# Two attention blocks on eight images: convolutions and layer 1's attention as seven half-size products, weight factors and the next image's q, k, v in DRAM, stages reordered

## The chip, the cores and the metric

The kernel runs on one core of a Trainium2 chip. Its time is the device time of one execution in microseconds (us), and the time of a version is the median of its runs. All arithmetic is in fp32.

## The reference

For each of 8 images x of 512 channels by 1024 positions, two blocks follow each other. Cut to what matters:

```
h  = group_norm(x, 32 groups)                 # layer 0
q, k, v = Wq h + bq, Wk h + bk, Wv h + bv     # 8 heads of 64 channels
a  = softmax(q^T k / 8, over keys) applied to v, per head
x  = x + Wp a + bp

h  = group_norm(x, 8 groups)                  # layer 1: one head of 512 channels
q, k, v = Wq h + bq, Wk h + bk, Wv h + bv
x  = x + Wp (softmax(q^T k / sqrt(512)) v) + bp
```

Each "W h" is a product of 512x512 by 512x1024; layer 0's attention multiplies 64 channels by 1024x1024 scores for each head, layer 1's 512 channels by 1024x1024.

## The kernel before, in words

A prologue, `fold`, multiplies layer 1's weights together once: M (`wm`) from those of q and k, Z (`wz`) from those of v and p. Layer 1 then needs g = M h, scores g^T h, z = Z h, and values from z. So an image has six convolutions: v, q, k and p with layer 0's weights, g and z with layer 1's. The weights stay in SBUF as four 128-row slices each (`KC` = 4). 128 is the height of the array, 512 columns (`HT`) is the width of one product and of one PSUM bank, and 128x512 is the unit in which products are counted here: 32 per convolution, 64 each for layer 1's scores and values. In the trace one fp32 product is two records.

PSUM has two pools: `ps_sc`, three tiles of two banks, for scores, convolutions and the `sums` of the softmax, and `ps_acc`, two tiles of one bank, for the running `av` and small products.

Layer 0's attention goes over 4 pairs of heads times 2 halves of the positions: 8 units per image. In a unit two parts follow each other, each with four score tiles (L300, two heads beside each other), four exponentials on ScalarE (L307), additions of these on VectorE (L309, L311) and four products with v into `av` (L320). A unit is ended during the next one: `reciprocals` sums the exponentials over the partitions with `ones` (L268), VectorE takes the reciprocal (L272) and keeps the largest sum (L274), GpSimd keeps the reciprocals' sum (L275); the reciprocals go through DRAM (L277) and come back to all partitions (L281) as r; VectorE multiplies `av` by r (L330).

The loop over images runs: attention of layer 0, p mixed with the next image's v, layer 1's normalization, g (`by_channel`, L223), z (`by_token`, L239), layer 1's attention in two halves (L347, L362), then the next image's q and k. p adds to x at L407. PSUM results leave alternately by VectorE and ScalarE. While attention of layer 0 runs, the next image's normalization is done as `extra`. A scheduler places the instructions on each engine, by the order in which the program gives them out and the tiles that become free; a few products of the next stage go ahead of waiting ones. DMAs are issued by SP, in the prologue by ScalarE too.

At the end, `top_sums` and `all_recs` decide whether a general path, which isn't run with these data, must do the work again.

Of the kernel before, what the change touches and what calls it, by code (L numbers as in the profile page):

```python
# [15 lines left out]
P = 128  # L16
EPS = 1e-5

# [9 lines left out]
def two_attention_blocks_kernel(  # L28
# [41 lines left out]
    wsb = [const.tile([P, KC, C], F32, name=f"w{i}") for i in range(4)]  # L70

    wm = const.tile([P, KC, C], F32, name="wm")
    wz = const.tile([P, KC, C], F32, name="wz")
# [3 lines left out]

    class GroupNorm:  # L80
        def __init__(self, layer, xt, uid):
            self.layer, self.xt, self.uid = layer, xt, uid
            self.mv = small.tile([P, KC, 2], F32, tag="mv", name=f"mv_{uid}")

        def stats(self, c):
            st = small.tile([P, 2, 6], F32, tag="bnst", name=f"bnst_{self.uid}_{c}")
            for i in range(2):
                nc.vector.bn_stats(st[:, i, :], self.xt[c][:, ts(i, HT)])
            nc.vector.bn_aggr(self.mv[:, c, :], st)
# [27 lines left out]
        def apply(self, engine, dst, c):  # L117
            engine.tensor_scalar(dst, self.xt[c], self.s[:, c : c + 1], self.b[:, c : c + 1], ALU.mult, ALU.add)  # L118

    def main_path(ctx):  # L120
        imgs = ctx.enter_context(tc.tile_pool(name="img", bufs=12))
# [3 lines left out]
        def img(name):  # L125
            return imgs.tile([P, T], F32, tag="img", name=name)

        def load_x(b, c, what):
            t = img(f"{what}_{b}_{c}")
            nc.sync.dma_start(t, x[b, c * P : (c + 1) * P, :])  # L130
            return t
# [6 lines left out]


        def fold():  # L140
            with tc.tile_pool(name="raw", bufs=1) as rawpool, tc.tile_pool(name="nat", bufs=2) as natpool:
                raw = [rawpool.tile([P, KC, C], F32, name=f"raw{i}") for i in range(4)]

                def load(i):
                    for h in range(2):
                        nc.scalar.dma_start(
                            raw[i][:, ts(h, 2), :],
                            w[4 + i, ts(h, C // 2), :].rearrange("(kc p) o -> p kc o", p=P),
                        )

                load(1)
                load(0)
                first = [load_x(0, c, "h0") for c in range(KC)]
                load(2)
                load(3)
                for i in (2, 0, 1, 3):
                    nc.scalar.dma_start(wsb[i], w[i].rearrange("(kc p) o -> p kc o", p=P))


                def natural(wt, nm):  # L160
                    t = natpool.tile([P, KC, C], F32, tag="nat", name=f"nat_{nm}")
                    for o in range(KC):
                        pt = acc_tile(f"tr_w{nm}_{o}")
                        for kc in range(KC):
                            nc.tensor.transpose(pt[:, ts(kc, P)], wt[:, kc, ts(o, P)], ident)
                        if o % 2 == 0:
                            nc.vector.tensor_copy(t[:, o, :], pt)
                        else:
                            nc.scalar.copy(t[:, o, :], pt)
                    return t  # L170

                def product(dst, lhs, rhs, nm):
                    for ic in range(KC):
                        ps = acc_tile(f"ps_w{nm}_{ic}")
                        for kc in range(KC):
                            nc.tensor.matmul(  # L176
                                ps, lhs[:, kc, ts(ic, P)], rhs[:, kc, :], start=(kc == 0), stop=(kc == KC - 1)
                            )
                        nc.vector.tensor_copy(dst[:, ic, :], ps)

                def bias_product(dst, lhs, vec, add, nm):
                    for oc in range(KC):
                        ps = acc_tile(f"ps_b{nm}_{oc}")
                        for kc in range(KC):
                            nc.tensor.matmul(
                                ps[:, 0:1], lhs[:, kc, ts(oc, P)], pcol(vec, kc), start=(kc == 0), stop=(kc == KC - 1)
                            )
                        if add is None:
                            nc.vector.tensor_copy(dst[:, oc : oc + 1], ps[:, 0:1])
                        else:  # L190
                            nc.vector.tensor_add(dst[:, oc : oc + 1], ps[:, 0:1], pcol(add, oc))

                wk = natural(raw[1], "k")
                wq = natural(raw[0], "q")
                norm = GroupNorm(0, first, "0_0")
                for c in range(KC):
                    norm.stats(c)
                product(wm, wq, wk, "m")
                norm.group_mean(acc_tile("gmean_0_0")[:, :KC])
                bias_product(ubias, wk, "bq1", None, "u")  # L200
                norm.affine(acc_tile("gvar_0_0")[:, :KC])
                for c in range(KC):
                    norm.apply(nc.vector if c % 2 else nc.gpsimd, first[c], c)
                product(wz, natural(raw[2], "v"), raw[3], "z")
                bias_product(obias[1], raw[3], "bv1", "bp1", "o")
                bias_product(obias[0], wsb[3], "bv0", "bp0", "o0")
            return first

        h0 = fold()
        qkpool = ctx.enter_context(tc.tile_pool(name="qka", bufs=16))  # L210
        vpool = ctx.enter_context(tc.tile_pool(name="vz", bufs=16))
        epool = ctx.enter_context(tc.tile_pool(name="e", bufs=6))
        sumpool = ctx.enter_context(tc.tile_pool(name="sum", bufs=2))
        rpool = ctx.enter_context(tc.tile_pool(name="r", bufs=2))
        rowpool = ctx.enter_context(tc.tile_pool(name="rows", bufs=3, space=bass.MemoryType.DRAM))


        def by_channel(wt, h, oc, bias, name):
            ps = sc_tile(f"ps_{name}")
            out = []  # L220
            for th in range(2):
                for kc in range(KC):
                    nc.tensor.matmul(  # L223
                        ps[:, th, :], wt[:, kc, ts(oc, P)], h[kc][:, ts(th, HT)], start=(kc == 0), stop=(kc == KC - 1)
                    )
                t = qkpool.tile([P, HT], F32, tag="qka", name=f"{name}_{th}")
                if th == 0:
                    nc.vector.tensor_scalar(t, ps[:, th, :], bias, None, ALU.add)
                else:
                    nc.scalar.activation(t, ps[:, th, :], AF.Identity, bias=bias)  # L230
                out.append(t)
            return out

        def by_token(wt, h, s2, name, between=None):
            ps = sc_tile(f"ps_{name}")
            out = []
            for i in range(2):
                for kc in range(KC):
                    nc.tensor.matmul(  # L239
                        ps[:, i, :], h[kc][:, ts(2 * s2 + i, P)], wt[:, kc, :], start=(kc == 0), stop=(kc == KC - 1)  # L240
                    )
                if i == 0 and between is not None:
                    between()
                t = vpool.tile([P, C], F32, tag="vz", name=f"{name}_{i}")
                if i == 0:
                    nc.vector.tensor_copy(t, ps[:, i, :])  # L246
                else:
                    nc.scalar.copy(t, ps[:, i, :])
                out.append(t)
            return out  # L250

        def queries_keys0(b, h):
            q, k = {}, {}
            for oc in range(KC):
                q[oc, 0], q[oc, 1] = by_channel(wsb[0], h, oc, pcol("bq0", oc), f"q0_{b}_{oc}")
                k[oc, 0], k[oc, 1] = by_channel(wsb[1], h, oc, pcol("bk0", oc), f"k0_{b}_{oc}")
            return q, k

        def reciprocals(total, heads, uid):

            sums = sc_tile(f"sums_{uid}").rearrange("p a b -> p (a b)")[:, : heads * P]
            sums = sums.rearrange("p (a b) -> p a b", a=heads)
            for i in range(4):
                nc.tensor.matmul(  # L268
                    sums[ts(i, 32), :, :], ones[:, :32], total[:, :heads, ts(i, P)], start=True, stop=True
                )  # L270
# [14 lines left out]
        def attention0(b, q, k, v, extra):  # L285
# [47 lines left out]
            while extra:  # L333
                extra.pop(0)()
# [279 lines left out]
```

## Time and profile before

| | |
|---|---|
| median of 3 runs | 3315.55 us (3313.39 to 3318.15) |
| profiled execution | 3314.92 us |
| its span | 3313.0 us |
| TensorE clock granted, mean | 0.995 |
| TensorE busy | 3257.4 us |
| VectorE busy | 1208.9 us |
| ScalarE busy | 658.1 us |
| GpSimd busy | 195.2 us |
| DMA | 81.82 MB, mean 25 GB/s |

The span is the time from the first to the last instruction that the profiler recorded. Busy time doesn't count register, branch, semaphore and DMA-issuing instructions. In the chain that ended last each step is followed back to what released it; "issue" in it is time in which the profile shows no wait. A row of the waits gives the engine and line that waited, the instruction on which it waited, the total in us, how often, and the longest. "DVE" is VectorE, "ACT" ScalarE, "PE" TensorE, "PEld" its weight loads, "POOL" GpSimd, "SP" the engine that issues DMAs.

### The profile page before, as it was taken

To read this page: it belongs to the slowest core of one execution; us is meant where nothing else is said; L and a number is where in the kernel's file an instruction comes from. 1 tells how busy PE (TensorE), PEld (TensorE's weight loads), DVE (VectorE), ACT (ScalarE), POOL (GpSimd) and SP (SyncE) were. 2 spreads that over 40 slices of the span, in tenths; PEclk is the share of its full clock that TensorE was granted. 3 is DMA by queue.
4 is the path that set the end of the run, shared out by engine and by line. 5 is a ranking of instruction groups with operands and counts; after the bars stand their busy time and mean duration, and the time that the engine had idled before them with its cause. 6 is when DMAs were issued, how large, how long until landed. Compare 5 with 4: busy or idle time off the path is not lost.

```text
span 3313.0 us, 24829 instructions
## 1 busy us (share of the span) xinstructions
PE 3257.4 (98%) x10130; PEld 1345.5 (41%) x10130; DVE 1208.9 (36%) x1461; ACT 658.1 (20%) x743; POOL 195.2 (6%) x149
## 2 busy tenths in 40 slices
PE   6999999999999999999999999999999999999899
PEld 3433444334443444434443344433444334443343
DVE  3165122751227412373124721256212651117512
ACT  0042001421014110240003400043000430005210
POOL 0010000100002000010000200010000100000000
PEclk9999999999999999999999999999999999999999
DMA  4000011000100002000020000100001000000000
GB/s 179 0 14 13 0 42 42 15 12 0 57 26 17 10 0 77 9 17 7 10 73 7 17 3 16 67 11 17 0 16 67 11 16 0 33 25 15 12 0 33
DMA packets 36697, 81.82 MB, mean 25 GB/s; under 512 B 5024, under 2 KB 5856, under 8 KB 36576
## 3 DMA queue, kind: packets, MB, share of 16 engines
q1 hardware_dynamic: 31872, 71.62, 6.3%
q10 hardware_dynamic: 4704, 8.55, 0.7%
q8 instruction: 82, 1.34, 0.2%
q14 instruction: 39, 0.32, 0.0%
HBM read 63.07 MB, written 17.07 MB: 24 GB/s over the span
## 4 chain that ended last, share of the span: by engine, by line
PE 93%; issue 4%; DVE 2%; POOL 0%; ACT 0%; DMA 0%; SPq 0%; DVEq 0%; ACTq 0%; POOLq 0%
PE av L362 13%; PE sc L347 13%; PE sc L300 13%; PE av L320 12%; PE ps_z L239 7%; PE ps_k L223 7%; PE ps_q L223 7%; PE ps_g L223 7%; PE ps_v L239 6%; PE ps_p L403 6%; PE sums L268 1%; DVE sum L311 1%; DVE sum L309 0%; PE ps_wz L176 0%; DVE h L118 0%
## 5 line engine op out<-in xcount | busy, mean ns | idle before, releaser
L307 ACT ACTIVATE e<-sc 128x1024 f32<-128x1024 f32 x512 | 484.5, 1029 | 479.3 <-PE sc L300 479.3
L311 DVE TENSOR_TENSOR sum<-sum,e 128x1024 f32<-128x1024 f32 x384 | 477.7, 1244 | 99.2 <-ACT e L307 77.9
L300 PE MATMUL sc<-q,k 64*128 64x512 f32 x2048 | 478.2, 603 | 7.6 <-DVE top_sums L274 7.6
L320 PE MATMUL av<-e,v 128*64 128x512 f32 x2048 | 467.7, 598 | 0.0
L362 PE MATMUL av<-e,z 128*128 128x512 f32 x1024 | 446.3, 594 | 0.0
L347 PE MATMUL sc<-g,h 128*128 128x512 f32 x1024 | 443.4, 592 | 0.0
L300 PEld LDWEIGHTS sc<-q,k 64*128 64x128 f32 x2048 | 186.4, 186 | 296.3 <-issue 239.4
L347 PEld LDWEIGHTS sc<-g,h 128*128 128x128 f32 x1024 | 194.6, 190 | 244.9 <-issue 244.9
L362 PEld LDWEIGHTS av<-e,z 128*128 128x128 f32 x1024 | 193.2, 190 | 240.4 <-issue 236.6
L275 POOL TENSOR_TENSOR all_recs<-all_recs,rc 128x256 f32<-128x256 f32 (+1 forms) x80 | 98.7, 1234 | 2628.6 <-DVE rc L272 1466.5
L320 PEld LDWEIGHTS av<-e,v 128*64 128x64 f32 x2048 | 135.6, 136 | 289.1 <-issue 251.7
L239 PE MATMUL ps_v<-w,h 128*128 128x512 f32 x512 | 239.2, 611 | 1.4 <-DVE v L246 1.4
L223 PE MATMUL ps_k<-h,w 128*128 128x512 f32 x512 | 236.2, 594 | 0.0
L223 PE MATMUL ps_q<-h,w 128*128 128x512 f32 x512 | 234.2, 592 | 0.0
L223 PE MATMUL ps_g<-h,wm 128*128 128x512 f32 x512 | 226.7, 599 | 3.5 <-DVE h L118 2.8
L239 PE MATMUL ps_z<-wz,h 128*128 128x512 f32 x512 | 229.1, 599 | 0.0
L403 PE MATMUL ps_p<-a,w 128*128 128x512 f32 x512 | 223.7, 592 | 0.8 <-DVE x L407 0.8
L352 ACT ACTIVATE e<-sc 128x1024 f32<-128x1024 f32 x64 | 65.5, 1023 | 595.2 <-PE sc L347 595.2
L223 PEld LDWEIGHTS ps_g<-h,wm 128*128 128x128 f32 x512 | 97.6, 192 | 129.4 <-issue 119.5
L239 PEld LDWEIGHTS ps_z<-wz,h 128*128 128x128 f32 x512 | 94.6, 190 | 131.3 <-issue 107.2
L403 PEld LDWEIGHTS ps_p<-a,w 128*128 128x128 f32 x512 | 97.1, 190 | 123.6 <-issue 121.2
L223 PEld LDWEIGHTS ps_k<-h,w 128*128 128x128 f32 x512 | 96.6, 190 | 124.7 <-issue 118.6
(88 smaller groups left out, 1329.6 us busy)
## 6 DMA issues: line engine op xcount, KB each, us to landing
h<-in_x SPq DMA_DIRECT2D x32, 512.0 KB
x<-in_x SPq DMA_DIRECT2D x32, 512.0 KB
r<-rows SPq DMA_DIRECT2D x128, 128.0 KB
out<-x SPq DMA_DIRECT2D x64, 256.0 KB
raw<-in_w ACTq DMA_DIRECT2D x8, 512.0 KB
w<-in_w ACTq DMA_DIRECT2D x4, 1024.0 KB
r<-rows SPq DMA_DIRECT2D x16, 256.0 KB
rows<-rc SPq DMA_DIRECT2D x64, 4.0 KB
```

The lines of the kernel that those rows point to most:

```text
L223: nc.tensor.matmul(ps[:, th, :], wt[:, kc, ts(oc, P)], h[kc][:, ts(th, HT)], start=(kc == 0), stop=(kc == KC - 1))
L239: nc.tensor.matmul(ps[:, i, :], h[kc][:, ts(2 * s2 + i, P)], wt[:, kc, :], start=(kc == 0), stop=(kc == KC - 1))
L268: nc.tensor.matmul(sums[ts(i, 32), :, :], ones[:, :32], total[:, :heads, ts(i, P)], start=True, stop=True)
L275: nc.gpsimd.tensor_tensor(all_recs[:, :heads, :], all_recs[:, :heads, :], rc, ALU.add)
L300: nc.tensor.matmul(sc[:, j, :], k[hp, s // 4][j * 64 : (j + 1) * 64, ts(s % 4, P)], q[hp, tb][j * 64 : (j + 1) * 64, :], start=True, stop= ...
L307: nc.scalar.activation(e, sc, AF.Exp, scale=(C // 8) ** -0.5)
L311: nc.vector.tensor_add(total, total, e)
L320: nc.tensor.matmul(av[j * 64 : (j + 1) * 64, :], v[s][:, hp * P + j * 64 : hp * P + (j + 1) * 64], es[s - part * NB][:, j, :], start=(s == ...
L347: nc.tensor.matmul(sc[:, i, :], h[kc][:, ts(2 * s2 + i, P)], g[kc, tb], start=(kc == 0), stop=(kc == KC - 1),)
L352: nc.scalar.activation(e, sc, AF.Exp, scale=C**-0.5)
L362: nc.tensor.matmul(ps, z[s][:, ts(c, P)], es[s // 2][:, s % 2, :], start=(s == 0), stop=(s == NS - 1))
L403: nc.tensor.matmul(ps[:, th, :], wsb[3][:, kc, ts(oc, P)], a[kc, th], start=(kc == 0), stop=(kc == KC - 1))
```

## The change

Every convolution, layer 1's scores and its values are cut into 2 by 2 blocks and computed with seven products of blocks in place of eight, after Strassen and Winograd. With blocks A of the left operand and B of the right one, sums are made of the blocks of each (`left_sums`, `right_sums`, 4 steps each for one tile pair), and of the seven products (`wino`). The products are given out in the order 1, 2, 6, 5, 7, 4, 3. Products 1 and 2 share tile a, 6, 7 and 4 accumulate in tile b, 5 and 3 in tile c; all three are `sc` tiles of two halves. Product 1 is copied to SBUF as t by ScalarE, t is added to 6 as u and to 7 as w by VectorE, and the four results are 1+2, c+w, b+t and c+u, written by `done`. Between products, a list of small steps, `background`, is run, two or three at a time, and hooks of the caller. Products by token write 256 columns each.

The left sums of the weights are made once, in the prologue and the first attention (`prepare`), are kept in DRAM (`keep`) and are loaded from there before every use (`load_weight`, 1.8 MB, three tiles). The new order is: attention of layer 0, the next image's v, p, the next image's q and k, g, scores, z, values. The next image's q, k and v are stored to DRAM and fetched again during values. x is read three times: for h, for the statistics, which are made during z one image ahead, and for the sum with p. One pool of 33 tiles of 128x1024 serves all of this. Layer 1's scores are made for all 1024 positions before z (`scores1`), and the exponentials' right sums are taken for the values. `reciprocals` takes its `sums` tile from the `acc` pool, which has two tiles, where it was from the `sc` pool. All DMAs are issued by SP.

The core of the diff (new functions, cut, and the loop):

```diff
+    def right_sums(lo, hi, t124, sub):
+        n = len(lo)
+        t1, t2, t4 = ([f(j) for j in range(n)] for f in t124)
+        b11, b12, b21, b22 = [l[0] for l in lo], [l[1] for l in lo], [h[0] for h in hi], [h[1] for h in hi]
+        steps = []
+        for j in range(n):
+            steps.append(lambda j=j: sub(t1[j], b12[j], b11[j]))
+            steps.append(lambda j=j: sub(t2[j], b22[j], t1[j]))
+            steps.append(lambda j=j: sub(b12[j], b22[j], b12[j]))
+            steps.append(lambda j=j: sub(t4[j], b21[j], t2[j]))
+        return {1: b11, 2: b21, 3: b22, 4: t4, 5: t1, 6: t2, 7: b12}, steps
...
+        def wino(uid, mm, done, order=(1, 2, 6, 5, 7, 4, 3), hooks=(), back=2):
+            bank = {1: "a", 2: "a", 6: "b", 7: "b", 4: "b", 5: "c", 3: "c"}
...
+            def upper(t, i, what):
+                t[i] = u_tile(what, i)
+                nc.vector.tensor_add(t[i], ps["b"][:, i, :], t1[i])
+            for p in order:
+                if bank[p] not in ps:
+                    ps[bank[p]] = sc_tile(f"ps{bank[p]}_{uid}")
+                for i in range(2):
+                    mm(p, i, ps[bank[p]][:, i, :], bank[p] not in ran)
+                    if p == 1:
+                        t1[i] = u_tile("t", i)
+                        nc.scalar.copy(t1[i], ps["a"][:, i, :])
+                    elif p == 2:
+                        done(i, 0, 0, ps["a"][:, i, :], None)
+                    elif p == 6:
+                        upper(u2, i, "u")
+                    elif p == 7:
+                        upper(u3, i, "w")
+                        done(i, 1, 1, ps["c"][:, i, :], u3[i])
+                    elif p == 4:
+                        done(i, 1, 0, ps["b"][:, i, :], t1[i])
+                    elif p == 3:
+                        done(i, 0, 1, ps["c"][:, i, :], u2[i])
+                ran.add(bank[p])
+                run_background(back)
...
+        def load_weight():
+            if uses:
+                n = uses.pop(0)
+                t = wpool.tile([P, 7, 2, C // 2], F32, tag="w", name=f"w_{n}_{len(uses)}")
+                nc.sync.dma_start(t, wdram[n])
+                loaded.append((n, t))
...
+        def by_channel(wf, hf, uid, done, **kw):
+            def mm(p, i, ps, start):
+                for k in range(2):
+                    nc.tensor.matmul(ps, wf[p][:, k, ts(i, P)], hf[p][k], start=start and k == 0, stop=k == 1, skip_group_check=True)
+            wino(uid, mm, done, **kw)
...
         def reciprocals(total, uid, across):
-            sums = sc_tile(f"sums_{uid}").rearrange("p a b -> p (a b)")[:, : heads * P]
+            sums = acc_tile(f"sums_{uid}")[:, : 2 * P].rearrange("p (a b) -> p a b", a=2)
...
+            a, ending = attention0(b, q, k, v, extra)
+            xt = [load_x(b, c, "x") for c in range(KC)]
+            af, steps = image_factors(a, f"a_{b}")
+            end = [ending, lambda: background.extend(steps)]
...
+                vn = by_token(weight("v"), hf0, f"v0_{b + 1}", hooks=[end])
+                load_weight()
+                store(2, vn)
...
+            by_channel(weight("p"), af, f"p_{b}", residual)
...
+                qn = conv(weight("q"), hf0, pcols("bq0"), f"q0_{b + 1}", hooks=[[mean], [], [affine], [normed]])
+                load_weight()
+                store(0, qn)
+                background.extend(steps1)
+                kn = conv(weight("k"), hf0, pcols("bk0"), f"k0_{b + 1}")
+                load_weight()
+                store(1, kn)
...
+            g = conv(weight("m"), hf1, ubias, f"g1_{b}")
...
+            e, total, ef = scores1(b, gf, hf1, f"1_{b}")
...
+            z = by_token(weight("z"), hf1, f"z1_{b}", hooks=[[], [], [], [], [sums]], back=3)
...
+            values1(b, zf, ef, state["r"], xt, f"1_{b}", hooks)
```

In the numbering of the changed kernel, t is copied at L223, u and w are added at L214, the products are at L292 (by channel), L304 (by token), L433 (scores) and L469 (values); in attention of layer 0 the scores are at L384, `av` at L404 and its multiplication by r at L413; in `reciprocals` the lines are L349 (sums), L351 (reciprocal) and L352 (maximum).

## The prediction

> **What bounds the kernel now.** I read the busy times first, then the chain that ended last, then TensorE's own waits.
>
> ```profile
> PE 3257.4 (98%) x10130; PEld 1345.5 (41%) x10130; DVE 1208.9 (36%) x1461; ACT 658.1 (20%) x743; POOL 195.2 (6%) x149
> PE 93%; issue 4%; DVE 2%; POOL 0%; ACT 0%; DMA 0%; SPq 0%; DVEq 0%; ACTq 0%; POOLq 0%
> ```
>
> TensorE is busy for 98% of a 3313.0 us span and carries 93% of the chain: only fewer, or cheaper, products make this kernel faster, and whatever makes TensorE wait adds to the time. Its waits are few:
>
> ```profile
> PE tr_wq L165 <- ACT nat_k L169: 13.0, 1, 13.0
> PE tr_wk L165 <- DMA raw<-in_w: 11.9, 2, 9.2
> PE sc L300 <- DVE top_sums L274: 7.6, 7, 1.4
> ```
>
> The first two are in the prologue. The third matters most here: 64 units of layer 0's attention take one `sums` tile each, and only 7 of them wait at all. The timeline around a boundary between two units tells why:
>
> ```profile
> 989.81 3.71 PE L300 MATMUL sc<-q,k 64*128 64x512 f32 x16
> 992.96 1.23 DVE L309 TENSOR_TENSOR sum<-e,e 128x1024 f32<-128x1024 f32 x1 [2.86 <-ACT e L307]
> 993.45 0.64 PE L268 MATMUL sums<-sum,ones 128*32 128x256 f32 x8
> 994.02 3.65 PE L320 MATMUL av<-e,v 128*64 128x512 f32 x16
> 994.29 1.23 DVE L311 TENSOR_TENSOR sum<-sum,e 128x1024 f32<-128x1024 f32 x1
> 995.43 1.75 DVE L272 RECIPROCAL rc<-sums 128x256 f32<-128x256 f32 x1
> 997.10 1.16 DVE L311 TENSOR_TENSOR sum<-sum,e 128x1024 f32<-128x1024 f32 x1
> 997.60 3.70 PE L300 MATMUL sc<-q,k 64*128 64x512 f32 x16
> 998.18 0.41 DVE L274 TENSOR_TENSOR top_sums<-sums,top_sums 128x256 f32<-128x256 f32 x1
> ```
>
> (Start, duration, engine, work.) The unit begins at 989.81, its four score pairs end at 993.45, `sums` of the unit before at 994.02, and `av` follows at once. The last reader of `sums` ends at 998.59, 8.78 us into the unit: VectorE puts additions between. Nobody on TensorE needs that tile so soon, as it is one of three score tiles.
>
> Rates from the timeline: a 128x512 product (two records) 0.858 us (64 records in 27.47), a pair of score products 0.909, a pair of `av` 0.896, `sums` 0.57. A unit is 8 x 0.909 + 8 x 0.896 + 0.57 = 15.0. One image is 400.3 us (from one image's first q to the next's). Before the first unit lie 169 us.
>
> **What the Trainium skill says.** (1) "TensorE: Matmul & The Clock Gate", LDWEIGHTS: a load goes by its columns, 107 ns for 128, and can go under the running product. The trace lists 190 ns, and beside 512 columns (429 ns a record) all is hidden; 256 columns (half of that, 214 ns) still cover it, barely. (2) The same page, Part 1: the clock falls after about one idle window of 3.4 us. Here the clock was 1.00 through gaps of 1.4 us, and 0.72 in 3130 to 3140, where gaps of 1.82, 0.84 and 2.79 follow each other. (3) Its "Architectural detail": VectorE and ScalarE take their work strictly in order; the timeline above agrees, so a late instruction holds all behind it. (4) "DMA: Bandwidth & Descriptors", Bandwidth: 341 GB/s at 1 MB, 425 at 16 MB; the prologue's loads here ran at 392 to 402.
>
> **The change, part by part.**
>
> *Fewer products.* Six convolutions, layer 1's scores and its values go from 32, 64 and 64 products (in units of 128x512) to 28, 56 and 56: 320 to 280 per image, 40 x 0.858 = 34.3 us, x 8 = 275 us. TensorE's work per image becomes 280 x 0.858 = 240.2, plus 8 x 14.44 of attention in layer 0, 8.5 x 0.57 of sums and some 2 of small products: 362.
>
> *The sums tile moves to the accumulator pool (two tiles).* One holds the running `av`, released only by the multiplication that waits for r; the other gets `sums` (L349). So the first `av` product (L404) of the next unit must wait for the last reader of `sums`, the maximum at L352: in the built order it does, in 7 of 8 units of each image. TensorE's order is scores 0 to 3, `sums`, scores 4 and 5, then that `av`. After `sums` (4.21 us into the unit) two score pairs take 1.82, so TensorE stands from 6.03. VectorE's order is as before (addition, addition, reciprocal, addition, maximum), so the maximum ends at 8.78 again; with 0.1 for restarting, the stall is 2.9 us. Behind the waiting `av` stand scores 6 and 7, so ScalarE has no more than two exps to do and catches up; later in the unit VectorE's additions come no later than before relative to `av`. No second wait grows: r, 5.2 us after the reciprocal, frees its tile at about 13.3 of 17.9, before the next `sums`. 7 x 2.9 = 20.3 us per image.
>
> *Waits inside a seven-product stage.* The tracking is per tile: each group (two products, 1.72 us) into a tile that ScalarE or VectorE is still reading for the group before waits for it. A 128x512 copy is 585 ns, an addition 691, biased 751; with 0.2 to start and 0.1 to restart the round trip is about 1.05, of which the one group in between, or its first product, hides 0.86. So 0.2 us for each of about 10 waits in each of 9 stages, more where VectorE has other work in front. Worked along each stage: v 1.1, p 0.5, q 2 (the mean waits for p's statistics), k 0.7, g 0.7, scores 1 and z 5.4 (VectorE is 81 to 100% full there with exponentials' sums, factors of e and g, statistics ahead), values 1.2, start of attention 0.4. Sum 12. If VectorE's reads were never late it is 0; the other end stands under the rivals.
>
> *VectorE's and ScalarE's extra work.* Factor sums (32 steps of 0.69 to 1.24), additions of partial products: VectorE rises from 148 to about 239 us per image, 60%. Hidden under TensorE but for what is counted above; without that cover it would be the 90 us.
>
> *DRAM traffic.* Seven weight factors (1.8 MB) per use, x three times, q, k, v stored (6.3 MB) and fetched: by the sizes of the tiles about 32 MB per image against 8. The fullest stretch is values 1: 12.3 MB of fetches, loads and stores in 48 us, 256 GB/s, under the 392 seen. All are issued by SP in order; the first tiles that attention needs are fetched first. SP's r transfers of layer 0 stand behind x's loads of 512 KB at most, and r has 4 us to spare. I put it at 0; without cover, 3 to 5 us for a late head of q, k or v per image (25 to 40 in all).
>
> *Sums for one image:* 362 + 20.3 + 12 = 394.5 against 400.3.
>
> *Prologue.* The 13.0 at `tr_wq` comes from ScalarE issuing loads, which SP now does: minus 13. Three convolutions: minus 10.3. Weight factors on VectorE and right-hand factors before the third product: plus 3 or so; bias products and product z change place, not size. 169 becomes about 145, +-15. Storing factors and loads stand in SP's queue behind x; nothing on TensorE waits for them before p.
>
> *Last image.* No v, q, k: 394.5 - 84 x 0.858 - 4 of their waits = 318, but their cover is gone: r, the factors of a (8 x 0.69), statistics, affine, application and the factors of h (8 x 0.69) come bare, about 18. 337. Tail 8.
>
> Sum: 145 + 7 x 394.5 + 337 + 8 = 3252. The profiled execution had 1.9 us outside its span and lay 0.6 below the median of the runs shown (3315.55), so I take **3250 us**, 65 less (2.0%).
>
> **Rivals.**
> A. The attention stall is not there, or is filled: 3250 - 8 x 20.3 = 3088. For it: a shift of the additions behind the maximum would be enough. Against: the dependency is in the order built, and VectorE's timing is measured.
> B. The seven-product stages cost much more: either the 256-column products of v and z (and the shorter ones) expose their weight loads, or VectorE's queue delays the reads. Slower than before from 0.036 us per record on 16 x 112 records, or 0.09 us more per wait on 720 waits. The products of one column for the biases run at 0.107 us per record: if all that were exposed, +190; if each read came 0.2 us later, +144. So 3390 to 3430. For it: VectorE is full around scores 1 and z. Against: 190 is below 214, and TensorE has a group in hand.
> C. The clock: 2.9 us is near the window. After the gaps at 3132 to 3136, 17 records took 9.91 instead of 7.30, so up to 2.6 lost, some of it waiting for h; at 1.7 for each of 56 stalls 3345. It decides from 1.2 us per stall. Against: TensorE was busy 83% of the unit, and one gap is shorter than the window.
> D. Fetches come late: 3275 to 3290, in the range of the forecast.
>
> **How the numbers follow.** Forecast with D 0.55 (own range 3200 to 3300), A 0.16 (3060 to 3150), B 0.19 (3300 to 3430), C 0.10 (3300 to 3395). The range 3110 to 3350 leaves out about half of A and half of B and C's upper ends. 0.2% is 6.6 us, what a measurement of this kernel can tell from no change. Faster: 0.52 + 0.16 + 0.03 = 0.71. Same 0.03. Slower 0.26.
>
> **What would show it.** TensorE busy near 8 x 362 + prologue, 2950 to 3000, and a largest wait "av <- DVE top_sums" of about 160 us in 56 times; mean 2.9. If that row is absent, A. Waits of the partial products on t, u and outputs together near 90; well over 150, or means of the 256-column records over half of 592, B. A clock under 0.97 in attention of layer 0, C. An image's period near 394. Waits of scores on fetched q or k would be D. The forecast is wrong if VectorE's order around the reciprocal differs from before on the chip, or if its 90 us more come in front of reads.

## The result, and the profile after

The changed kernel takes 3323.85 us (median of 4 runs, 3322.19 to 3326.96) against 3315.07 for the kernel before (the three runs of the table above and one more). The ratio is 1.0027, with a 95% interval from 1.0009 to 1.0044: 0.3% slower, where 2.0% faster was forecast. The profiled execution took 3322.55 us, with a span of 3320.8 and a mean TensorE clock of 0.977 (0.995 before).

First the busy times and the chain of the changed kernel, as shown of the kernel before:

```profile
PE 3121.7 (94%) x10322; PEld 1400.5 (42%) x10322; DVE 1831.2 (55%) x2445; ACT 765.0 (23%) x925; POOL 145.4 (4%) x119
PE 81%; DVE 8%; issue 7%; ACT 3%; DMA 0%; POOL 0%; SPq 0%; DVEq 0%; ACTq 0%; POOLq 0%
```

TensorE is busy 136 us less, not 275, and VectorE now carries 8% of the chain. TensorE's waits (engine and line, what it waited for: us in total, times, longest; the rows cut are of the prologue and the last image, or of 1.1 us or less):

```profile
PE av L404 <- DVE top_sums L352: 152.1, 56, 3.1
...
PE psa_sc L433 <- ACT t_sc L223: 5.8, 8, 0.7
PE psa_sc L433 <- ACT e L441: 5.5, 8, 0.7
...
```

The stall in layer 0's attention is there, in 56 units, 2.72 us in the mean. All the partial products together wait for little (about 16 us). So the products saved and the stall are much as forecast, and something else is missing. It is in the timeline of TensorE over two units that follow each other (start, duration, work; in brackets the idle time before, and what ended it):

```profile
975.76 0.64 PE L349 MATMUL sums<-sum,ones 128*32 128x256 f32 x8
976.33 1.99 PE L384 MATMUL sc<-q_again,k_again 64*128 64x512 f32 x8
981.05 3.65 PE L404 MATMUL av<-e,v_again 128*64 128x512 f32 x16 [2.73 <-DVE top_sums L352]
984.63 1.99 PE L384 MATMUL sc<-q_again,k_again 64*128 64x512 f32 x8
...
993.77 0.64 PE L349 MATMUL sums<-sum,ones 128*32 128x256 f32 x8
994.34 1.99 PE L384 MATMUL sc<-q_again,k_again 64*128 64x512 f32 x8
999.06 5.35 PE L404 MATMUL av<-e,v_again 128*64 128x512 f32 x16 [2.73 <-DVE top_sums L352]
1004.34 1.99 PE L384 MATMUL sc<-q_again,k_again 64*128 64x512 f32 x8
```

Both units stand for 2.73 us. After it, the same sixteen `av` records take 3.58 us in the first (981.05 to 984.63) and 5.28 in the second (999.06 to 1004.34): 1.70 more. The clock granted in the two units (busy time and instructions by engine, then PEclk, share of the DMA engines, GB/s):

```profile
975.70:993.70 18.00, 15.27 (x74) 5.32 (x72) 11.02 (x11) 7.65 (x9) 1.51 (x1) 1.00 0.06 16
993.70:1013.40 19.70, 16.97 (x74) 5.80 (x72) 11.22 (x11) 7.65 (x9) 1.51 (x1) 0.91 0.04 14
```

The clock was 1.00 in the first and 0.91 in the second. Of the 56 stalls, 33 are followed by such a slow `av` (5.1 to 5.3 us, the rest 3.6): 33 x 1.70 = 56 us, which busy time counts as work.

### The profile page after: what moved, and what is told of

Its sections match the earlier page's. It is cut to its first block, busy times and chain, and to the rows that moved or that the text cites. A ratio compares the mean times of both kernels' runs of the same rounds, so it can differ in the third digit from the quotient of the medians.

```text
span 3320.8 us, 26890 instructions
## 1 busy us (share of the span) xinstructions
PE 3121.7 (94%) x10322; PEld 1400.5 (42%) x10322; DVE 1831.2 (55%) x2445; ACT 765.0 (23%) x925; POOL 145.4 (4%) x119
## 2 busy tenths in 40 slices
DMA packets 78295, 283.55 MB, mean 85 GB/s; under 512 B 9360, under 2 KB 16336, under 8 KB 71632
## 4 chain that ended last, share of the span: by engine, by line
PE 81%; DVE 8%; issue 7%; ACT 3%; DMA 0%; POOL 0%; SPq 0%; DVEq 0%; ACTq 0%; POOLq 0%
PE av L404 16%; PE sc L384 8%; PE psb_av L469 5%; PE psb_sc L433 5%; PE psa_av L469 3%; PE psc_av L469 3%; PE psb_v L304 3%; PE psa_sc L433 3%; PE psb_g L292 3%; PE psb_k L292 3%; PE psb_q L292 3%; PE psb_z L304 3%; PE psc_sc L433 2%; ACT e L391 2%; DVE sum L395 2%
## 5 line engine op out<-in xcount | busy, mean ns | idle before, releaser
L404 PE MATMUL av<-e,v_again 128*64 128x512 f32 x1792 | 458.2, 658 | 133.1 <-DVE top_sums L352 133.1
L384 PE MATMUL sc<-q_again,k_again 64*128 64x512 f32 x1792 | 450.7, 609 | 0.0
L404 PEld LDWEIGHTS av<-e,v_again 128*64 128x64 f32 x1792 | 143.0, 148 | 436.1 <-issue 400.4
L384 PEld LDWEIGHTS sc<-q_again,k_again 64*128 64x128 f32 x1792 | 165.9, 186 | 262.5 <-issue 213.9
L353 POOL TENSOR_TENSOR all_recs<-all_recs,rc 128x256 f32<-128x256 f32 x72 | 96.3, 1337 | 1831.4 <-DVE rc L351 1831.4
L351 DVE RECIPROCAL rc<-sums 128x256 f32<-128x256 f32 x72 | 125.9, 1748 | 23.3 <-PE sums L349 23.3
L433 PE MATMUL psa_sc<-g,h 128*128 128x512 f32 x256 | 125.4, 602 | 11.7 <-ACT t_sc L223 5.8
L413 DVE TENSOR_TENSOR a<-av,r 128x512 f32<-128x512 f32 x64 | 44.2, 691 | 162.7 <-DMA r<-rows 158.5
L469 PE MATMUL psa_av<-e,z 128*128 128x512 f32 x256 | 120.1, 601 | 0.0
L404 PE MATMUL av<-e,v 128*64 128x512 f32 x256 | 66.3, 665 | 19.0 <-DVE top_sums L352 19.0
L433 PEld LDWEIGHTS psa_sc<-g,h 128*128 128x128 f32 x256 | 46.7, 190 | 81.3 <-issue 47.8
L292 PE MATMUL psa_g<-h,w_m 128*128 128x512 f32 x128 | 66.7, 636 | 4.0 <-ACT h L129 3.3
L469 PEld LDWEIGHTS psa_av<-e,z 128*128 128x128 f32 x256 | 46.7, 190 | 53.2 <-issue 40.1
L384 PE MATMUL sc<-q,k 64*128 64x512 f32 x256 | 68.1, 622 | 0.0
L304 PE MATMUL psa_z<-w_z,h 128*128 128x256 f32 x256 | 64.6, 385 | 0.0
L214 DVE TENSOR_TENSOR u_sc<-psb_sc,t_sc 128x512 f32<-128x512 f32 x32 | 22.1, 691 | 76.6 <-PE psb_sc L433 76.6
L433 PE MATMUL psc_sc<-sg,h 128*128 128x512 f32 x128 | 63.6, 599 | 0.6
```

The lines of the kernel that those rows point to most:

```text
L292: nc.tensor.matmul(ps, wf[p][:, k, ts(i, P)], hf[p][k], start=start and k == 0, stop=k == 1, skip_group_check=True)
L304: nc.tensor.matmul(ps[:, ts(jj, C // 2)], hf[p][k][:, ts(2 * i + jj, P)], wf[p][:, k, :], start=start and (jj, k) == (0, 0), stop=(jj, k) ...
L351: nc.vector.reciprocal(rc, sums)
L353: nc.gpsimd.tensor_tensor(all_recs, all_recs, rc, ALU.add)
L384: nc.tensor.matmul(sc[:, j, :], k[hp][j * 64 : (j + 1) * 64, ts(s, P)], q[hp][j * 64 : (j + 1) * 64, ts(tb, HT)], start=True, stop=True,)
L404: nc.tensor.matmul(av[j * 64 : (j + 1) * 64, :], v[s // 2][:, s % 2, hp * P + j * 64 : hp * P + (j + 1) * 64], es[s - part * NB][:, j, :], ...
```

## The experiments

Two theories at first. The main one: one tile placement, `sums` in the accumulator pool, costs both the stall (152 us) and the clock's fall (56). The rivals: the clock falls because of the new seven-product stages, or a stall of any length costs it.

**`sums` from the score pool again**, in the changed kernel:

```diff
-            sums = acc_tile(f"sums_{uid}")[:, : 2 * P].rearrange("p (a b) -> p a b", a=2)
+            sums = sc_tile(f"sums_{uid}").rearrange("p a b -> p (a b)")[:, : 2 * P]
+            sums = sums.rearrange("p (a b) -> p a b", a=2)
```

> The changed kernel with one edit: `sums` comes from the score pool again, as before the change. Theory: the accumulator tile causes the 56 stalls (152 us) and each long stall lets the clock fall for one stretch of 3.41 us (33 times 1.70 = 56 us). Then the row `av <- DVE top_sums` is gone, the mean clock is back near 0.995, and the time is 3323 - 152 - 56 = about 3115, plus up to 8 for scores that wait for the tile instead, as in the kernel before: 3115 to 3125. Rival 1, the clock falls for another reason: the stalls go and the 56 stay, about 3171. Rival 2, the wait only moves to the three score tiles, which the seven-product stages need as well: over 3200.

Measured: 3143.73 us, ratio 0.9487 (0.9472 to 0.9503), clock 0.993. The row `av <- DVE top_sums` is gone, and so is nearly all of the clock's fall; both rivals fall. It is 19 us above the upper end of the forecast, and the first wait of TensorE in this run is large enough for that:

```profile
PE sums L350 <- DVE sum L396: 28.7, 17, 4.0
```

`sums` now waits for the last addition of its unit. One such place, in the timeline of this run:

```profile
1004.20 0.69 DVE L414 TENSOR_TENSOR a<-av,r 128x512 f32<-128x512 f32 x1 [5.03 <-DMA r<-rows]
1004.81 2.54 DVE L396 TENSOR_TENSOR sum<-sum,e 128x1024 f32<-128x1024 f32 x2
1007.27 0.69 DVE L164 TENSOR_TENSOR t_h<-h,t_h 128x512 f32<-128x512 f32 x1
1007.87 1.22 DVE L396 TENSOR_TENSOR sum<-sum,e 128x1024 f32<-128x1024 f32 x1
1009.01 0.69 DVE L164 TENSOR_TENSOR t_h<-h,t_h 128x512 f32<-128x512 f32 x1
1009.61 1.22 DVE L396 TENSOR_TENSOR sum<-sum,e 128x1024 f32<-128x1024 f32 x1
1010.97 0.64 PE L350 MATMUL sums<-sum,ones 128*32 128x256 f32 x8 [2.12 <-DVE sum L396]
```

VectorE stood 5.03 us for r with four additions queued behind its multiplication, and then took two subtractions for the next image's h among them. The long units of the changed kernel had left room for this: no wait of `sums` for an addition is among its rows.

**The same edit alone in the kernel before:**

```diff
-            sums = sc_tile(f"sums_{uid}").rearrange("p a b -> p (a b)")[:, : heads * P]
+            sums = acc_tile(f"sums_{uid}")[:, : heads * P]
```

> The kernel before with that one edit of the change alone: `sums` from the accumulator pool. Theory: the same 7 stalls an image of about 2.7 us, and the clock falls after some 6 in 10 of them: 3315 + 153 + 56 - 8 = about 3515. Rival 1 (the clock's fall belongs to the seven-product stages): 3460. Rival 2 (the stall needs the new stages around it): 3315.

Measured (two runs): 3547.14 us, ratio 1.0703 (1.0681 to 1.0724), clock 0.977.

```profile
PE av L320 <- DVE top_sums L274: 145.2, 49, 4.3
PE av L320 <- DVE gmean L96: 16.9, 7, 2.4
```

56 stalls again (seven end on a small product of the normalization, which takes the same pool), and 39 of them are followed by a slow `av`, 64.5 us. So neither the stall nor the clock's fall needs the new stages. It is 32 us above the expectation: seven stalls are 4.3 us, the clock costs 8.5 more, and a unit with a stall of 2.73 and no slow clock takes 18.01 in the changed kernel, 0.28 more than 15.0 and the stall.

**Shorter stalls: no maximum over `sums` in layer 0's attention.**

```diff
-            nc.vector.tensor_tensor(top_sums, sums, top_sums, ALU.max)
+            if across:
+                nc.vector.tensor_tensor(top_sums, sums, top_sums, ALU.max)
```

> The changed kernel without the maximum over `sums` in layer 0's attention (this leaves out the check of the largest sum there). The last reader of `sums` is then the reciprocal; in the built order one and a half score pairs stand ahead of `av`, so the stall should be about 1.9 us. Theory with a clock that looks at free-running stretches of 3.413 us and halves the next one when over about 2.05 us of a stretch was idle (fitted to the 56 stalls of the changed kernel): 1.9 is under it, none of 56 slow; 3323 - 56 x 0.83 - 56 = about 3220. Rival, each stall has the same chance to cost clock whatever its length: 33 of 56 slow, 3276.

Measured: 3241.02 us, ratio 0.9779 (0.9763 to 0.9795), clock 0.992.

```profile
PE av L405 <- DVE rc L351: 74.5, 56, 1.9
...
1007.53 1.98 PE L385 MATMUL sc<-q_again,k_again 64*128 64x512 f32 x6
1011.41 5.35 PE L405 MATMUL av<-e,v_again 128*64 128x512 f32 x16 [1.90 <-DVE rc L351]
```

48 of the stalls are 1.24 to 1.3 us, and none of these is followed by a slow `av`; of the eight of 1.6 to 1.9, six are. So not every stall costs clock, and the rival's 33 of 56 falls; but the theory's none of 56 was missed as well. A unit became only 0.65 us shorter (17.36 instead of 18.01), not 1.5 as the row would say. The six score records ahead of the stall tell why. They are one score pair and a single product of the next pair. The records of a pair, four in all, start two by two and take 0.91 us; those of the single product follow each other, 0.43 us apart, and so do those of its partner, which comes after `av`. The split pair takes 2 x 0.86 in place of 0.91, 0.81 more, and of the 1.49 by which the stall is shorter 0.68 is left. The sum fits the span: 56 x 0.65 + 27 x 1.70 = 82, and it went from 3320.8 to 3239.8.

**Longer stalls: the maximum taken four times.**

```diff
-            nc.vector.tensor_tensor(top_sums, sums, top_sums, ALU.max)
+            for _ in range(1 if across else 4):
+                nc.vector.tensor_tensor(top_sums, sums, top_sums, ALU.max)
```

> The changed kernel with the maximum over `sums` taken four times in layer 0's attention (the result is the same; VectorE works 1.2 us more per unit). The tile is released later, but the scheduler then puts five score pairs ahead of the waiting `av` instead of two. Theory (what counts is how long TensorE stands, not when the tile is free): stall about 1.3 us, no slow stretch, 3323 - 56 x 1.4 - 56 = about 3190. Rival, the release sets the time: 3323 + 56 x 1.2 = 3390.

Measured: 3432.87 us, ratio 1.0356 (1.0339 to 1.0373), clock 0.955. My expectation fell, and the rival was near (3390). In 24 units five score pairs did go ahead, but VectorE put three further additions between the four maxima, which I had not looked at:

```profile
1034.80 0.41 DVE L353 TENSOR_TENSOR top_sums<-sums,top_sums 128x256 f32<-128x256 f32 x1
1035.13 1.21 DVE L396 TENSOR_TENSOR sum<-sum,e 128x1024 f32<-128x1024 f32 x1
1036.26 0.41 DVE L353 TENSOR_TENSOR top_sums<-sums,top_sums 128x256 f32<-128x256 f32 x1
```

These stalls are 4.7 to 5.3 us. In the other 32 the four maxima stand together, but only three pairs (12 records) go ahead, and the stall is 3.2 to 3.3 us:

```profile
1008.75 2.85 PE L385 MATMUL sc<-q_again,k_again 64*128 64x512 f32 x12
1014.84 5.35 PE L405 MATMUL av<-e,v_again 128*64 128x512 f32 x16 [3.25 <-DVE top_sums L353]
```

The stalls are 219.3 us in all. The run serves as the long end: after each of the 56, `av` is slow, 108 us together. In the changed kernel and these two variants the share of stalls that cost clock goes with their length: none of 48 at 1.24 to 1.3, six of eight at 1.6 to 1.9, 33 of 56 at 2.5 to 3.1, all 56 at 3.2 and more.

**`sums` in the accumulator pool, but copied out at once by ScalarE.**

```diff
+            held = rpool.tile([P, 2, P], F32, tag="held", name=f"held_{uid}")
+            nc.scalar.copy(held, sums)
+            sums = held
```

> The changed kernel with `sums` still in the accumulator pool, but copied to SBUF by ScalarE at once; reciprocal and maximum read the copy. Theory: not the pool matters but how late the last reader comes. ScalarE can copy at about 5.5 us into the unit, TensorE is free at 5.1: gaps under 0.6 us, none slow. 3323 - 56 x 2.5 - 56 = about 3127, plus what the run with `sums` in the score pool has shown to come next (sums that wait for a late addition, 25 to 30): 3125 to 3155. Rival, two accumulator tiles are too few whoever reads: over 3250.

Measured: 3194.82 us, ratio 0.9626 (0.9609 to 0.9642), clock 0.988. The wait of `av` for the maximum is gone from the rows with two accumulator tiles, so the late last reader made the stall, and not the number of tiles alone. What comes next is larger than with the score pool:

```profile
PE sums L349 <- DVE sum L398: 66.6, 32, 5.2
```

VectorE's additions are placed otherwise here, and again four of them stand behind the multiplication that waits for r. I had taken 25 to 30 for this from the other run; it is 38 us more, and the run missed the upper end of its expectation by 40.

**What is left: GpSimd takes the eight subtractions of h** (`sums` in the score pool; the diff is cut to the call):

```diff
...
-                hf0, steps = image_factors(h0, f"h0_{b + 1}")
+                hf0, steps = image_factors(h0, f"h0_{b + 1}", nc.gpsimd.tensor_sub)
```

> The run with `sums` in the score pool, and the eight subtractions for the next image's h in layer 0's attention on GpSimd instead of VectorE. Theory: the 28.7 us in which `sums` waited for the last addition come from these subtractions, which stand among the additions when r is late: 17 waits become the few of the kernel before (2 us), with some slow clock gone, 3144 - 25 to 30 = about 3115. Rival 1, r alone is too late: 3140. Rival 2, GpSimd is too slow and v waits for its factors, or it slows VectorE: over 3150.

Measured: 3132.44 us, ratio 0.9441 (0.9425 to 0.9457), 17 us above the expectation. The wait went from 28.7 to 18.4 us, and 5.7 of waits for exponentials came with it: the subtractions were only a part. The same edit with the copy by ScalarE:

> Both edits: `sums` copied out of the accumulator tile by ScalarE, and the eight subtractions on GpSimd. Theory: as the run with `sums` in the score pool and GpSimd's subtractions, about 3115, or a few us less, as no score tile is taken; rival: ScalarE's copies in front of exponentials cost what the tile gives, 3125 or more.

Measured: 3171.77 us, ratio 0.9566 (0.9550 to 0.9582), against the expectation: `sums` still waits 52.2 us for additions. The score pool is the better place in both pairs; why the additions come later with the copy was not isolated.

**The multiplication by r leaves VectorE's queue**, on top of the run with GpSimd's subtractions:

```diff
-                        r = reciprocals(total, uid, False)
-                        nc.vector.tensor_mul(a[hp][:, ts(tb, HT)], av, r)
+                        half = a[hp][:, ts(tb, HT)]
+                        nc.scalar.copy(half, av)
+                        r = reciprocals(total, uid, False)
+                        nc.gpsimd.tensor_mul(half, half, r)
```

> The run with `sums` in the score pool and GpSimd's subtractions, and in layer 0's attention ScalarE copies `av` to SBUF while GpSimd multiplies it there by r. Theory: what is left of the waits of `sums` (18.4 us, mostly at the last unit of an image, and 5.7 for exponentials) comes from the multiplication that waits for r in VectorE's queue, with four additions behind it. Then they fall to a few us: 3132 - 20, 3110 to 3118. Rival 1: the additions are late because VectorE has too much to do, not because of the waiting: 3125 to 3132. Rival 2: ScalarE's copy delays exponentials: over 3132.

Measured: 3111.57 us, ratio 0.9381 (0.9365 to 0.9396), as the theory had it. The largest waits of TensorE after its first transposes' load are now:

```profile
PE psa_sc L436 <- ACT e L444: 5.9, 8, 0.7
PE psb_z L304 <- DVE w_z L214: 5.9, 16, 0.8
PE psa_sc L436 <- ACT t_sc L223: 5.8, 8, 0.7
```

`sums` waits for an addition only once more, for 0.3 us, so the multiplication in VectorE's queue was the cause of what was left. The edit takes away its wait for r (5.03 us in the place shown) and its own 0.69 us of work per unit; this run doesn't separate the two, and the wait is the larger. This version beats both kernels: 6.2% less than before the change, 6.4% less than after it.

## Why the prediction was wrong

The range (3110 to 3350) held the time only because it was drawn wide for the rivals; the main forecast's own range ended at 3300, and the direction was wrong. Point by point, by the prediction's own steps:

- *Fewer products*: right. Between the end of layer 0's attention and the next one's start lie 255.6 us (1105.60 to 1361.20), with 245.0 of work by the prediction's rates (280 products 240.2, score pairs drawn ahead 3.1, small products 1.7). With `sums` back in the score pool the change is worth 171 us, and 203 with VectorE's queue in order, of the 275. TensorE's busy time, forecast as 2950 to 3000, is 3058.6 with `sums` back: products that start late (below) count as busy, an estimated 8 x 9.3 us.
- *The sums tile moves to the accumulator pool*: right in place, count and size. 56 stalls of 2.72 us, 152 us, where 2.9 and 162 were forecast. The undone edit shows that it is the cause.
- *Waits inside a seven-product stage*: right in the sum, and partly by luck. 255.6 - 245.0 = 10.6 us per image, 12 forecast. But the rows of waits show only about 16 us in the whole run, 11 of them for scores 1, where the prediction looked for near 90. The rest is in 97 records of this stretch that start about a tenth late, 9.3 us together. Only about a third of them follow a read by VectorE or ScalarE that has just ended, and the kernel before has 112 late starts in an image too (attention included), so they are not shown to be the waits that were forecast.
- *VectorE, DRAM*: hidden, as said. VectorE is busy for 1831.2 us (55%); no wait of TensorE for a fetched q, k, v or a weight factor shows, though 283.55 MB were moved.
- *Prologue and last image*: 153 us and 350 with the tail, where 145 and 345 were forecast. The prologue's 8 us were not traced further.
- *The clock*: this is the step that failed. The forecast had it at nothing, and a rival, C, had the mechanism and the 1.7 us per stall with a chance of 0.10. It was argued away with two reasons: TensorE busy for 83% of a unit, and a gap shorter than the 3.4 us that the Trainium skill names. Neither holds: gaps of 1.6 to 3.1 us do it in 39 of 64 cases, and each time 1.70 us is lost. The sign set for C, a clock under 0.97 in attention of layer 0, came: it is 0.95 from 958.57 to 1105.60. The trace before had a hint of it: in the stretch 3130 to 3140 that the prediction cites, the clock fell to 0.72 with no gap longer than 2.79 us.

The sum now, against the forecast span of 3252: + 56 of clock, - 10 of stall, + 8 of prologue, + 15 of smaller terms (most of it 0.28 us for each stalled unit, which the stall alone doesn't tell) = 3321, and the span was 3320.8. The gain forecast was 65, so the 56 of the clock alone would have left about nothing.

Of the other rivals, A was ruled out by the row of 56 waits, and B by the 10.6 us. The sign set for B's columns was a bad one: means of the 256-column records over half of 592 ns. They are 379 to 389, over half, and yet nothing is exposed, since a listed record is longer than the distance to the next start (592 listed, 429 apart):

```profile
1117.45 3.19 PE L304 MATMUL psc_v<-w_v,t_h 128*128 128x256 f32 x14
1120.47 1.89 PE L304 MATMUL psb_v<-w_v,h 128*128 128x256 f32 x8
```

The 14 records take 3.02 us to the next start, 216 ns each, half of 429. (The one-column products that B was priced with start 0.112 us apart in the trace, not 0.107.)

## What to carry to other kernels

When a tile moves to another pool, write down for that pool who holds each buffer at the moment when the next one is asked for, and when its last reader comes: the change of one line here cost 180 us net, as much as the seven-product form had brought. Don't price a stall of TensorE at its own length alone: here one of 1.3 us or less cost no clock, one of 2.5 to 3.1 cost 1.70 us more in 33 of 56 cases, and one of 3.2 or more always cost clock. And ask what the stall was covering: here it hid a multiplication that stood for 5 us at the head of VectorE's queue, worth, together with eight subtractions, another 32 us once the stall was gone.

## What the runs showed of the hardware

The clock's fall was sharper than I had expected. "TensorE: Matmul & The Clock Gate" in the Trainium skill, Part 1, says that the clock halves after an idle window of about 3.4 us, in windows that run free of the program. The traces keep the granted clock as well, and they agree with the second half. In all ten kernels it is 1.00 or 0.50 and nothing between, and within a run all half-clock stretches start whole multiples of 3.413 us apart; each of the 33 in the changed kernel's stalled units is one such window long. On this grid the two units shown above come apart (stretch and its length, TensorE's busy time and records, PEclk, share of the DMA engines, GB/s):

```profile
976.09:979.50 3.41, 2.23 (x16) 1.00 0.00 0
979.50:982.92 3.42, 1.87 (x10) 1.00 0.07 19
...
996.57:999.98 3.41, 0.92 (x6) 1.00 0.00 1
999.99:1003.39 3.40, 3.40 (x12) 0.50 0.24 82
```

The stall of 2.73 us is the same in both. In the first unit it falls across two windows, which are idle for 1.18 and 1.55 us, and the clock stays. In the second it puts 2.49 us into one window, and the next window runs at half clock; the 1.70 us lost is half of a window. So it goes in the whole changed kernel outside the prologue: every window at full clock with 2.06 us idle or more is followed by one at half clock, and none with 2.01 or less. In the kernel before with the moved tile the two limits are 2.08 and 2.05. An estimate from this: a stall of 2.73 us puts over 2.05 us into one window in 60% of its possible positions, and 33 of 56 is 59%.

This stands against the first half of the skill's statement: a window need not be idle throughout. The limit of 2.05 us isn't the whole rule either. In the run without the maximum, windows with 1.59 and 1.76 us idle were followed by half clock, and one with 1.87 was not; there a single score product, which uses 64 of the array's 128 rows, stands ahead of the stall. Whether that counts as half idle no run here tests.

A stall also changes what busy time means. The changed kernel's TensorE shows 3121.7 us busy, and 3058.6 with the stall removed and not one product fewer.
